# Statistics on ScalarE, a residual added by transfers, an earlier chain of token sums and a split last block

## The chip, the cores and the metric

The kernel runs on one core of a Trainium2 chip. The metric is the device time of one execution in microseconds (us), here the median of several executions. Engines are named as in the profile: PE multiplies matrices (PEld is its weight load), DVE is VectorE, ACT is ScalarE, POOL is GpSimd, SP is SyncE, which here only issues DMA transfers.

## The reference

Two batches of 1024 tokens, D = 1024 columns, all in fp32:

```
xn  = layernorm(x)                               # per token over D
s   = xn @ (weight with 32x32 blocks masked).T + bias
c_b = softmax(Wq @ mean_tokens(xn_b) . keys)     # 8 mixing weights per batch
y   = xn @ (W_org + sum_e c_b[e] * down_e up_e).T
out = x + s * silu(y)
```

## The kernel before, in words

**Precision.** Every fp32 operand is kept as a rounded part and a remainder ("hi" and "lo", made by an ACT cast and a DVE subtraction), and each product is three matmuls: L425, L426, L427 for the batch-0 products, L389, L390, L391 for the mixing of the weights, L1147 for batch 1.

**Order of work.** The order on PE, DVE, ACT and POOL is that of the source, written by hand. Each of these engines runs its instructions in that order. Only SP's queue, from which nearly all loads go out, is ordered by a scheduler. So an instruction that waits holds all that is behind it on its engine.

**Stages.** Batch 0 is worked through in eight tiles of 128 tokens and two halves of 512 output columns:

- a start that loads, normalises and transposes batch 0 and computes the products with half 0 of the masked matrix (`s0`);
- the loop over k that mixes half 0 of the batch-0 matrix `y00`. For each of eight row tiles: `y_prep` splits a tile of the down matrices (`dhi` L380 on ACT, `dlo` L381 on DVE), `y_mul` is 12 matmuls into a `psw` bank (L389 to L391; there are two banks), `y_sum` adds W_org on DVE (L396), `y_hi` (L399, ACT) and `y_lo` (L407, DVE) split the sum. The `cut` tiles (L367 ACT, L368 DVE) are the up matrices times the mixing weights;
- `phase("y", 0, 0, ...)`, eight tiles of 24 matmuls (`gemm`) each followed by a `y_mul` for `y01`; `jobs_b` lists the side work per tile: stores, `mask_part` (block mask sums), `nat_stats` (mean and variance of a batch-1 token tile with two `bn_stats` L144 and an aggregate on DVE), `spread_stats` (spreads them into rows), and the first steps of the wide chain;
- `phase("y", 0, 1, ...)`, eight tiles of 24 matmuls; `jobs_c` makes the rows of `s1`, the other half of the masked matrix (load `ws`, L274 DVE, L277 ACT, L282 DVE), goes on with the wide chain, and computes the mixing weights of batch 1 (`coeffs(1)`);
- `s_tile(0..7)`, eight tiles with `s1`, with the 16 mixing steps of batch 1 (`fold`) between the first five;
- batch 1 by a scheme of seven products per 2x2 block (`quad` over eight units of 84 matmuls, L1147), whose token operands are the sums and differences of token tiles prepared by the wide chain. ACT copies (L1178, L1154 for `s5` and `s2`, L1202) and DVE adds move partial sums between banks. `out_tile` finishes a block (L1124 to L1134).

**The wide chain.** `wide_load(j, half)` loads 512 KB of transposed batch-1 tokens, `wide_a(j)` and `wide_b(j)` normalise the first and the second of a pair, and `wide_b` also forms the sums and stores them to DRAM (`xv`) from POOL's queue. There are four pairs.

**Residuals of batch 0.** For each final tile SP loads the input tile into `res` ahead of the products; after them DVE multiplies by the `stash` (L471) and adds to `res` (L472); `store_late` puts the store on ACT's queue (L480). In batch 1 the same sum is made for most blocks by a transfer of POOL that adds the input to the block in place (L1130), and by a DVE add (L1133) in the last unit.

**The end.** The last unit's three last products go into `pb`, `py` and `pa`, one bank each; each is followed by two 128x512 operations of DVE (L1124, L1133) and a store.

Of the kernel before, what the change touches and what calls it, by code (L numbers as in the profile page):

```python
# [9 lines left out]
F32 = mybir.dt.float32  # L10
# [3 lines left out]
AF = mybir.ActivationFunctionType  # L14
ALU = mybir.AluOpType
# [17 lines left out]
def kernel(  # L33
# [130 lines left out]
    def nat_stats(b, i):  # L164
        t = b * TPB + i
        xn = nat_tile()
        nc.sync.dma_start(xn, x[t * P : (t + 1) * P, :])
        bn(t, xn, 0)
        bn(t, xn, 1)
        rstd_of(t)  # L170

    def group(b, g):
        if (b, g) not in xg:
# [287 lines left out]
            y_evac(mine, ps, b, i)  # L461
        stash[(b, h, i)] = mine

    def final_evac(kind, b, h, i, ps, res):
        t = b * TPB + i
        mine = stage_l.tile([P, NH], F32, name="mine", tag="g", bufs=2)
        if kind == "s":
            s_evac(mine, ps, b, i, h * NH, NH)
        else:
            y_evac(mine, ps, b, i)  # L470
        nc.vector.tensor_tensor(mine, mine, stash[(b, h, i)], ALU.mult)  # L471
        nc.vector.tensor_tensor(res, res, mine, ALU.add)  # L472
        late_stores.append((out[t * P : (t + 1) * P, h * NH : (h + 1) * NH], res))

    late_stores = []

    def store_late():

        while late_stores:
            nc.scalar.dma_start(*late_stores.pop(0))  # L480

    sum_stores = []

# [12 lines left out]
    def phase(kind, b, h, w, final, jobs):  # L496

        for i in range(TPB):
            t = b * TPB + i
            if final:  # L500
                res = stage_l.tile([P, NH], F32, name="res", tag="res", bufs=3)
                nc.sync.dma_start(res, x[t * P : (t + 1) * P, h * NH : (h + 1) * NH])
            flush()
            if (b, h, i) in split_at:
                ps, part = open_gemm(b, i, w)
                part(0, 4)
                split_at[(b, h, i)]()
                part(4, NKT)
            else:
                ps = gemm(b, i, w)  # L510
            if final:
                pending.append(J(final_evac, kind, b, h, i, ps, res))
            else:
                pending.append(J(tile_evac, kind, b, h, i, ps))
            for job in jobs(i):
                job()
# [100 lines left out]
    with tc.manual_schedule(engines={mybir.EngineType.PE, mybir.EngineType.DVE, mybir.EngineType.Activation, mybir.EngineType.Pool}):  # L617
# [208 lines left out]
        for k in range(NKT):  # L826
            y_mul(0, 0, k)
            if k == 0:
                tile_evac("s", 0, 0, 7, q7)
            y_sum(0, 0, k)  # L830
            if k + 2 < NKT:
                y_prep(0, 0, k + 2)
            y_hi(y00, 0, 0, k)
            y_lo(y00, 0, 0, k)

        def mix_jobs(dst, b, h, i):
            if i == 0:
# [13 lines left out]
        def jobs_b(i):  # L851
            if i == 0:
                yield J(scale_up, 0, 1)
            yield J(mix_jobs, y01, 0, 1, i)
            yield J(store_late)
            if i < 4:
                yield J(mask_part, 2 + i // 2, i % 2)
            for t in ((0,), (1, 2), (3, 4), (5,), (6, 7), (), (), ())[i]:
                yield J(nat_stats, 1, t)
            if i == 4:  # L860
                yield J(wide_load, 0, 0)
                yield J(wide_load, 0, 1)
            if i == 5:
                yield J(spread_stats)
                yield J(wide_a, 0)
            if i == 6:
                yield J(wide_b, 0)
            if i == 7:
                yield J(wide_load, 1, 0)
                yield J(wide_load, 1, 1)  # L870


# [20 lines left out]
        def wide_load(j, half):  # L893
            if half == 0:
                pair = lambda n: cupool.tile([P, 2, NH], F32, name=n, tag="cu")
                if j == 0:
                    tt = [stash_p.tile([P, NH], F32, name="tt", tag="stash") for _ in range(2)]
                    wide[0] = pair("ac"), tt, nat_tile().rearrange("p (g n) -> p g n", g=2)
                elif j == 1:
                    ac, bd, tt = pair("ac"), pair("bd"), pair("tt")  # L900
                    wide[1] = ac, [tt[:, 0], tt[:, 1]], bd
                elif j == 2:
                    tt = pair("tt")
                    wide[2] = wide[0][0], [tt[:, 0], tt[:, 1]], wide[0][2]
                else:
                    wide[3] = wide[1]
            kt = j + 4 * half
            t = wide[j][2 * half]
            nc.sync.dma_start(t.rearrange("p g n -> p (g n)"), xT[kt * P : (kt + 1) * P, S : 2 * S])
# [36 lines left out]
        steps = coeffs(1)  # L946

        def jobs_c(i):
            if i == 6:
                yield steps[0]  # L950
                yield steps[1]
            if i == 7:
                yield steps[3]
                yield J(scale_up, 1, 0)
            yield J(s_mul, s1, 1, i)
            yield J(s_lo, s1, 1, i)
            if i in (1, 3):
                yield J(wide_load, (i + 3) // 2, 0)
                yield J(wide_load, (i + 3) // 2, 1)
            if i < 6:  # L960
                yield J((wide_a, wide_b)[i % 2], 1 + i // 2)

        split_at[(0, 1, 7)] = steps[2]
        phase("y", 0, 1, y01, False, jobs_c)


# [38 lines left out]
        ORDER_X = (0, 3, 4, 1, 5, 2, 6)  # L1005

        def s_tile(i):
            res = stage_l.tile([P, NH], F32, name="res", tag="res", bufs=3)
            nc.sync.dma_start(res, x[i * P : (i + 1) * P, NH:])
            store_late()  # L1010
            flush()
            ps = gemm(0, i, s1)
            pending.append(J(final_evac, "s", 0, 1, i, ps, res))

        units = [("s", 0), ("y", 0), ("y", 1), ("s", 1), ("y", 2), ("s", 2), ("y", 3), ("s", 3)]
        opools = [None, None]
# [88 lines left out]
        held = {}  # L1105
        pools_b1 = {}

        def out_tile(u, i, t, ps):

            kind, p = units[u]  # L1110
            n = p + 4 * i
# [1 line left out]
            if u % 2 == 0:  # L1113
# [3 lines left out]
                else:  # L1117
                    nc.scalar.activation(g, ps, AF.Silu)
                gates[(p, i, t)] = g
                return  # L1120
            g = gates.pop((p, i, t))
            res = held.pop((i, t), None)
# [17 lines left out]
                nc.sync.dma_start(res, xT[n * P : (n + 1) * P, S + t * NH : S + (t + 1) * NH])  # L1140
                held[(i, t)] = res

        def product(u, a, m, ps, start, js=range(4)):
            o = ow[u]
            for j in js:
                for k, (wl, xl) in enumerate(((0, 0), (0, 1), (1, 0))):
                    nc.tensor.matmul(  # L1147
                        ps, lhsT=o[:, a, wl, j, :], rhs=xw[j][:, m, xl, :],
                        start=start and j == 0 and k == 0, stop=j == 3 and k == 2, skip_group_check=True,
                    )  # L1150

# [5 lines left out]
        def quad(u, ahead, behind=()):  # L1157
# [41 lines left out]
            slot(3)  # L1199
            product(u, 2, 5, pb, False)  # L1200
            after(4)
            nc.scalar.copy(pa, pb)  # L1202
            nc.vector.tensor_tensor(pb, pb, s5, ALU.add)
            slot(4)
            product(u, 6, 2, py, False)
            out_tile(u, 0, 1, py)
            out_tile(u, 1, 1, pb)
            res_load(u, 1, 0)
            slot(5)
            product(u, 3, 6, pa, False)  # L1210
            out_tile(u, 1, 0, pa)
# [9 lines left out]
        cm_t2, pools_b1["tmp2"] = open_pool("tmp2", 1)  # L1221
        ahead = unit_jobs(1)
        behind = [[J(fill, j, m, xs_pool) for j in (2, 3)] for m in ORDER_X[2:]]
        behind[1].insert(0, store_late)
        quad(0, ahead, behind)
        close(cm_xs)
        cm_t, pools_b1["tmp"] = open_pool("tmp", 1, side="right")
# [59 lines left out]
```

## Time and profile before

| what | value |
|---|---|
| median of 3 executions | 461.38 us (459.7 to 463.19) |
| the profiled execution | 462.08 us |
| its span, first to last instruction | 460.1 us |
| mean granted clock of PE | 0.986 |
| PE, DVE, ACT, POOL busy | 97%, 66%, 37%, 13% |
| instructions | 5752 |
| moved by DMA | 89.52 MB, 195 GB/s on average |
| accumulating transfers of batch 1 | 12 of 256 KB, 6.1 us from issue to landing |
| stores of batch 0 | 16 of 256 KB, 2.7 us |
| loads of `ws` | 8 of 256 KB, 5.5 us |

The span is counted from the first to the last instruction; the execution's time contains it and 1.98 us around it. The busy time of an engine says how much it had to do, not what set the end; that is read from waits, from the chain of work that ended last, and from the granted clock in stretches of the span. A row of a timeline gives start, length, engine, line, operation, output and inputs, and in brackets the engine's idle time just before with what ended it. A matmul of 128x512 shows a length of 0.39 us in a row, but matmuls overlap: the next one starts 0.227 us later.

### The profile page before, as it was taken

How to read it: one execution, taken by the hardware profiler on the slowest of the kernel's cores; microseconds unless marked ns; L12 is line 12 of the kernel's file. 1: busy time of each engine (PE TensorE's matmuls, PEld its weight loads, DVE VectorE, ACT ScalarE, POOL GpSimd, SP SyncE). 2: the span in 40 equal slices, each digit the busy share in tenths (PEclk: the TensorE clock that was granted, in tenths of full speed). 3: DMA queues.
4: the chain of work that ended last, by engine and by line, in shares of the span. 5: the costliest groups of instructions: out<-in, count | busy, mean ns of one | idle time of the engine just before them, and what ended most of it. 6: DMA issues, size and time to landing. Idle time of an engine off the chain costs nothing.

```text
span 460.1 us, 5752 instructions
## 1 busy us (share of the span) xinstructions
PE 444.7 (97%) x2047; PEld 365.4 (79%) x2047; DVE 305.1 (66%) x492; ACT 169.3 (37%) x277; POOL 59.5 (13%) x72
## 2 busy tenths in 40 slices
PE   7799999999999999997999999999999999999995
PEld 5689888888887888885888788877888888888884
DVE  5889778666775788866546776669466294465624
ACT  3576624363323132213324233158243422441510
POOL 3764210000010202230000000000020020002000
PEclk9899999999999999997999999999999999999999
DMA  8995406687862586799778985664274246218003
GB/s 267 390 350 196 146 24 205 183 281 255 287 230 93 186 317 227 277 309 303 243 249 276 297 274 152 207 219 137 79 147 134 85 98 177 91 24 220 31 1 114
DMA packets 47404, 89.52 MB, mean 195 GB/s; under 512 B 4752, under 2 KB 14992, under 8 KB 47376
## 3 DMA queue, kind: packets, MB, share of 16 engines
q1 hardware_dynamic: 32784, 70.28, 46.1%
q0 software_dynamic: 3840, 10.49, 8.9%
q10 hardware_dynamic: 10752, 8.39, 5.7%
q8 instruction: 16, 0.26, 0.2%
q14 instruction: 12, 0.10, 0.1%
HBM read 69.21 MB, written 19.92 MB: 194 GB/s over the span
## 4 chain that ended last, share of the span: by engine, by line
PE 85%; DVE 8%; DMA 4%; issue 1%; ACT 1%; SPq 0%; ACTq 0%; DVEq 0%
PE acc_ps L1147 23%; PE acc_ps L425 11%; PE acc_ps L426 11%; PE acc_ps L427 11%; PE py L1147 9%; PE psw L391 6%; PE psw L389 6%; PE psw L390 6%; DMA ws<-in_wT_dram 2%; DMA raw<-in_x_dram 1%; DVE slot L558 1%; DVE ramp L549 1%; DMA misc<-in_up_dram 1%; DVE st L144 1%; DVE xw L1002 1%
## 5 line engine op out<-in xcount | busy, mean ns | idle before, releaser
L1147 PE MATMUL acc_ps<-xw,ow 128*128 128x512 f32 x480 | 113.6, 393 | 0.4 <-ACT acc_ps L1178 0.4
L425 PE MATMUL acc_ps<-slot,xgrp 128*128 128x512 f32 (+1 forms) x288 | 107.4, 373 | 2.8 <-ACT slot L277 2.7
L426 PE MATMUL acc_ps<-slot,xgrp 128*128 128x512 f32 (+1 forms) x288 | 106.8, 371 | 2.7 <-DVE slot L558 2.7
L427 PE MATMUL acc_ps<-slot,xgrp 128*128 128x512 f32 (+1 forms) x288 | 106.4, 369 | 0.7 <-DVE xgrp L570 0.7
L1147 PEld LDWEIGHTS acc_ps<-xw,ow 128*128 128x128 f32 x480 | 90.0, 188 | 21.3 <-ACT acc_ps L1178 0.8
L426 PEld LDWEIGHTS acc_ps<-slot,xgrp 128*128 128x128 f32 x288 | 54.9, 191 | 12.6 <-DVE slot L558 3.6
L425 PEld LDWEIGHTS acc_ps<-slot,xgrp 128*128 128x128 f32 x288 | 54.8, 190 | 12.3 <-ACT slot L277 3.1
L427 PEld LDWEIGHTS acc_ps<-slot,xgrp 128*128 128x128 f32 x288 | 55.0, 191 | 10.2 <-DVE xgrp L570 1.1
L391 PE MATMUL psw<-cut,dlo 128*128 128x512 f32 x128 | 50.9, 397 | 0.8 <-DVE dlo L381 0.8
L389 PE MATMUL psw<-cut,dhi 128*128 128x512 f32 x128 | 51.0, 399 | 0.0
L390 PE MATMUL psw<-cut,dhi 128*128 128x512 f32 x128 | 50.6, 395 | 0.0
L1147 PE MATMUL py<-xw,ow 128*128 128x512 f32 x192 | 46.9, 392 | 0.0
L1147 PEld LDWEIGHTS py<-xw,ow 128*128 128x128 f32 x192 | 36.1, 188 | 8.1
L1047 DVE TENSOR_TENSOR ow<-raw,ow 128x1024 fp32r<-128x1024 f32 (+1 forms) x32 | 34.5, 1087 | 10.4 <-ACT ow L1046 10.4
L1130 POOL DMA_DIRECT2D gate<-in_xT_dram x12 | 10.5, 906 | 203.0 <-DVE gate L1128 133.9
L380 ACT CAST dhi<-ds 128x512 fp32r<-128x512 f32 x32 | 19.8, 617 | 40.0 <-PE psw L390 23.8
L396 DVE TENSOR_TENSOR wo<-wo,psw 128x512 f32<-128x512 f32 x32 | 22.0, 686 | 18.6 <-PE psw L391 18.5
L1046 ACT CAST ow<-raw 128x1024 fp32r<-128x1024 f32 (+1 forms) x32 | 29.4, 940 | 1.6 <-DVE wo L396 1.6
L391 PEld LDWEIGHTS psw<-cut,dlo 128*128 128x128 f32 x128 | 24.5, 192 | 6.7 <-DVE dlo L381 1.2
L390 PEld LDWEIGHTS psw<-cut,dhi 128*128 128x128 f32 x128 | 24.6, 192 | 5.4
L389 PEld LDWEIGHTS psw<-cut,dhi 128*128 128x128 f32 x128 | 24.6, 192 | 5.2
L1192 DVE TENSOR_TENSOR py<-py,s 128x512 f32<-128x512 f32 x8 | 5.6, 698 | 30.7 <-ACT s L1154 30.7
(160 smaller groups left out, 477.6 us busy)
## 6 DMA issues: line engine op xcount, KB each, us to landing
ds<-in_down_dram SPq DMA_DIRECT2D x32, 256.0 KB, 3.7
wo<-in_worgT_dram SPq DMA_DIRECT2D x32, 256.0 KB, 3.8
raw<-in_x_dram SPq DMA_DIRECT2D x11, 512.0 KB, 6.5
res<-in_x_dram SPq DMA_DIRECT2D x16, 256.0 KB, 3.8
out_dram<-res ACTq DMA_DIRECT2D x16, 256.0 KB, 2.7
raw<-in_wu_dram SPq DMA_DIRECT2D x8, 512.0 KB, 5.1
yu<-wo ACTq DMA_DIRECT2D x16, 256.0 KB, 4.1
xs<-xv SPq DMA_DIRECT2D x16, 256.0 KB, 4.0
```

The source lines that it names most:

```text
L380: nc.scalar.copy(dhi, ds)
L389: nc.tensor.matmul(ps, lhsT=dhi[:, c, :], rhs=u[c][:, 0, :], start=c == 0, stop=False)
L390: nc.tensor.matmul(ps, lhsT=dhi[:, c, :], rhs=u[c][:, 1, :], start=False, stop=False)
L391: nc.tensor.matmul(ps, lhsT=dlo[:, c, :], rhs=u[c][:, 0, :], start=False, stop=c == 3)
L396: nc.vector.tensor_tensor(ws, ws, ps, ALU.add)
L425: nc.tensor.matmul(ps, lhsT=xs[:, kt, 0, cols], rhs=w[:, kt, 0, wc], start=kt == 0, stop=False)
L426: nc.tensor.matmul(ps, lhsT=xs[:, kt, 0, cols], rhs=w[:, kt, 1, wc], start=False, stop=False)
L427: nc.tensor.matmul(ps, lhsT=xs[:, kt, 1, cols], rhs=w[:, kt, 0, wc], start=False, stop=kt == NKT - 1)
L1046: nc.scalar.copy(o[:, a:b, 0], raw[:, a:b])
L1047: nc.vector.tensor_tensor(o[:, a:b, 1], raw[:, a:b], o[:, a:b, 0].bitcast(F32), ALU.subtract)
L1130: nc.gpsimd.dma_start(g, xT[n * P : (n + 1) * P, S + t * NH : S + (t + 1) * NH], accum_op=ALU.add)
L1147: nc.tensor.matmul(ps, lhsT=o[:, a, wl, j, :], rhs=xw[j][:, m, xl, :], start=start and j == 0 and k == 0, stop=j == 3 and k == 2, skip_gro ...
```

## The change

1. `act_stats` computes a batch-1 tile's mean and variance with ACT: a copy that also sums, two small DVE operations for the mean and its negative, a square with the negative mean as bias that also sums, a small DVE operation and POOL's power. Three tiles are done in the y00 loop after k = 2, 4 and 6, two more in tiles 0 and 1 of phase y(0,0); the other three stay with `nat_stats`.
2. `final_evac` multiplies into the stash tile, adds the input by an accumulating DMA from POOL's queue, and `store_out` stores the tile from ACT's queue later. The `res` tiles of batch 0 and their loads are gone.
3. The steps of the wide chain move one tile to the front; its second pair gets other buffers; `coeffs(1)` and `scale_up(1, 0)` move from tiles 6 and 7 to 5 and 6 and `s_mul`/`s_lo` of rows 5 to 7 are all put into tile 5's jobs.
4. In the last unit, the order of the finished blocks is changed and the last product is done in two halves of 256 columns in two banks, each half with its own two DVE operations and store.

```
+    def act_stats(i):
+        t = TPB + i
+        xn = nat_tile()
+        nc.sync.dma_start(xn, x[t * P : (t + 1) * P, :])
+        sm = small.tile([P, 2], F32, name="sm2")
+        nc.scalar.activation(xn, xn, AF.Copy, accum_out=sm[:, 0:1])
+        m = small.tile([P, 2], F32, name="mean1", bufs=5)
+        nc.vector.tensor_scalar(m[:, 0:1], sm[:, 0:1], 1.0 / D, None, ALU.mult)
+        nc.vector.tensor_scalar(m[:, 1:2], sm[:, 0:1], -1.0 / D, None, ALU.mult)
+        nc.scalar.activation(xn, xn, AF.Square, bias=m[:, 1:2], accum_out=sm[:, 1:2])
+        ve = small.tile([P, 1], F32, name="ve", bufs=3)
+        nc.vector.tensor_scalar(ve, sm[:, 1:2], 1.0 / D, EPS, ALU.mult, ALU.add)
+        nc.gpsimd.tensor_tensor(rstd[:, t : t + 1], ve, mhalf, ALU.pow)
+        means[t] = m[:, 0:1]
...
-        nc.vector.tensor_tensor(mine, mine, stash[(b, h, i)], ALU.mult)
-        nc.vector.tensor_tensor(res, res, mine, ALU.add)
-        late_stores.append((out[t * P : (t + 1) * P, h * NH : (h + 1) * NH], res))
+        res = stash[(b, h, i)]
+        nc.vector.tensor_tensor(res, res, mine, ALU.mult)
+        t = b * TPB + i
+        at = slice(t * P, (t + 1) * P), slice(h * NH, (h + 1) * NH)
+        nc.gpsimd.dma_start(res, x[at], accum_op=ALU.add)
+        out_stores.append((out[at], res))
...
             y_hi(y00, 0, 0, k)
             y_lo(y00, 0, 0, k)
+            if k in (2, 4, 6):
+                act_stats(k // 2 - 1)
... jobs_b
-            yield J(store_late)
+            yield J(store_out, 1)
             if i < 4:
                 yield J(mask_part, 2 + i // 2, i % 2)
-            for t in ((0,), (1, 2), (3, 4), (5,), (6, 7), (), (), ())[i]:
+            if i < 2:
+                yield J(act_stats, 3 + i)
+            for t in ((), (5,), (6,), (7,), (), (), (), ())[i]:
                 yield J(nat_stats, 1, t)
+            if i == 3:
+                yield J(wide_load, 0, 0)
             if i == 4:
-                yield J(wide_load, 0, 0)
                 yield J(wide_load, 0, 1)
-            if i == 5:
                 yield J(spread_stats)
                 yield J(wide_a, 0)
+            if i == 5:
+                yield J(wide_b, 0)
+                yield J(wide_load, 1, 0)
             if i == 6:
-                yield J(wide_b, 0)
+                yield J(wide_a, 1)
             if i == 7:
-                yield J(wide_load, 1, 0)
                 yield J(wide_load, 1, 1)
... jobs_c
-            if i == 6:
+            if i < 2:
+                yield J(store_out, 1 - i)
+            if i == 5:
                 yield steps[0]
                 yield steps[1]
-            if i == 7:
+            if i == 6:
                 yield steps[3]
-                yield J(scale_up, 1, 0)
-            yield J(s_mul, s1, 1, i)
-            yield J(s_lo, s1, 1, i)
-            if i in (1, 3):
-                yield J(wide_load, (i + 3) // 2, 0)
-                yield J(wide_load, (i + 3) // 2, 1)
+                yield J(scale_up, 1, 0, up_homes)
             if i < 6:
-                yield J((wide_a, wide_b)[i % 2], 1 + i // 2)
-        split_at[(0, 1, 7)] = steps[2]
+                yield J(s_mul, s1, 1, i)
+                yield J(s_lo, s1, 1, i)
+            if i == 5:
+                for kt in (6, 7):
+                    yield J(s_mul, s1, 1, kt)
+                    yield J(s_lo, s1, 1, kt)
+            if i in (0, 2):
+                yield J(wide_load, 2 + i // 2, 0)
+                yield J(wide_load, 2 + i // 2, 1)
+            if i < 5:
+                yield J((wide_b, wide_a)[i % 2], 1 + (i + 1) // 2)
+        split_at[(0, 1, 6)] = steps[2]
... quad, last unit
+                out_tile(u, 1, 1, pb)
+                res_load(u, 1, 0)
+                product(u, 6, 2, py, False)
+                out_tile(u, 0, 1, py)
+                for c, pc in halves:
+                    product(u, 3, 6, pc, False, cols=c)
+                    out_tile(u, 1, 0, pc, c)
+                return
... quad(0)
-        behind[1].insert(0, store_late)
+        behind[2].insert(0, store_out)
```

## The prediction

> **What bounds the kernel now.** I read the page's first section, then the windows of each stage, the chain that ended last, and last the timelines of the engines at the edited places.
>
> ```profile
> PE 444.7 (97%) x2047; PEld 365.4 (79%) x2047; DVE 305.1 (66%) x492; ACT 169.3 (37%) x277; POOL 59.5 (13%) x72
> ...
> L425 PE MATMUL acc_ps<-slot,xgrp 128*128 128x512 f32 (+1 forms) x288 | 107.4, 373 | 2.8 <-ACT slot L277 2.7
> ```
>
> The matmul engine is busy in all but 15 us. The change removes no product, so it can win only what the matmul engine waits or runs slowly, some of the 15 us and the tail, and it can lose wherever it makes that engine wait. The second line already names the largest single wait, 2.7 us behind L277, a row of the matrix s1. The windows show it with what it drags behind it (columns: stretch, its length, busy time and count of PE, PEld, DVE, ACT, POOL, then granted clock, DMA share, GB/s):
>
> ```profile
> 205.00:210.00 5.00, 5.00 (x23) 3.85 (x21) 3.61 (x8) 2.68 (x4) 0.08 (x1) 1.00 1.02 393
> 210.00:215.00 5.00, 2.27 (x6) 1.50 (x6) 2.61 (x5) 2.23 (x4) 0.00 (x0) 0.71 0.89 268
> 215.00:220.00 5.00, 5.00 (x15) 3.95 (x14) 2.52 (x5) 0.62 (x1) 0.00 (x0) 0.60 0.65 211
> ```
>
> The granted clock falls to a half after the wait. A 128x512 matmul follows the one before it after 0.23 us at full clock and 0.43 at half, as the chain that ended last shows (start, us, what):
>
> ```profile
> 200.81 0.61 DVE ws L274
> ...
> 202.82 8.54 DMA ws<-in_wT_dram
> 211.38 0.70 DVE ws L274
> 212.11 0.63 ACT slot L277
> 212.74 0.04 issue
> 212.78 0.80 PE acc_ps L425
> ...
> 218.57 0.43 PE psw L389
> ...
> 219.26 0.23 PE psw L391
> ```
>
> The last ws tile was issued at 202.82, took 8.54 us beside 393 GB/s of other loads, and after two casts s_tile(0) could go on. The matmul before it started at 209.66, so its slot ended at 209.89: 2.89 us idle. From 212.4 to 219.0 the engine issued 15 matmuls in 6.56 us, where full clock takes 15 x 0.227 = 3.40: 3.16 lost. Together 6.05 us.
>
> **Part 1: token pairs one tile sooner.** Now jobs_c runs the chain wide_a, wide_b, each over one 512 KB load, to tile 5 of phase y(0,1); it ends at 198.8, 38.3 us after that phase began at 160.5, and ws, coeffs(1) and its wu loads crowd behind it. In the built order one pair more is done in phase y(0,0), the chain has five steps left, and bd(1), issued behind the last y_mul of y(0,0), lands about 5.2 us into the phase. From there five steps and the s_mul and s_lo between them are 27.7 us of DVE work by their rows: end at +32.9, 5.4 sooner. The ws loads of rows 5 to 7 are then issued at +29.5 to +30.3 and land, at 5.5 to 8.54 us each, at +35 to +39. Rows 5 to 7, soft and the cuts follow in DVE's order; the first dlo of y(1,0) comes out at +49.0 to +50.5 and is wanted at +50.15. So 0 to 2 us of wait remain, I take 0.3, and with a wait that short the clock loss goes too: -5.7 (-4 to -6.05).
>
> **Part 2: residual by accumulating transfers.** Sixteen res loads leave SP and sixteen adds of 0.69 us leave DVE (11.1 us); sixteen accumulating DMAs come onto POOL, and each store on ACT now waits for one. The nearest row is batch 1's accumulates (line, engine op, count, KB each, median us to landing):
>
> ```profile
> gate<-in_xT_dram POOLq DMA_DIRECT2D x12, 256.0 KB, 6.1
> ```
>
> Each also holds POOL about 0.91 us to issue (L1130). In y(0,0) a tile is 8.16 us, and ACT and POOL are mostly idle: nothing lost, since a store is issued one tile late. In the folds one matmul wait can be read, 0.78 us at 255.4 to 256.2, where dlo (L381) came late on DVE right behind the res add of 252.51. One add less in that chain shrinks it by 0.69: -0.7 (0 to -0.8).
>
> The price lies in quad(0). There the store of tile 7 stands in ACT's order ahead of two fills and of the copy s2, and product(2,5), which writes the bank that s2 reads, waits for s2.
>
> ```profile
> 299.55 1.56 PE L1147 MATMUL acc_ps<-xw,ow 128*128 128x512 f32 x6
> ...
> 305.72 7.61 PE L1147 MATMUL acc_ps<-xw,ow 128*128 128x512 f32 x31 [0.41 <-ACT acc_ps L1178]
> ```
>
> ```profile
> 307.60 0.58 ACT L1154 COPY s<-py 128x512 f32<-128x512 f32 x1
> 309.64 1.25 ACT L1001 CAST xw<-xs 128x512 fp32r<-128x512 f32 x2 [1.46 <-DMA xs<-xv]
> 310.80 0.58 ACT L1154 COPY s<-acc_ps 128x512 f32<-128x512 f32 x1
> ```
>
> Tile 7's last matmul starts at 299.32; its product with the stash is done near 304.3, and at 6.1 us the accumulate lands at 310.4 (4.6 to 8.6 us seen, less part of the issue: 309.3 to 313). Then two fills of 0.62 each and the copy of 0.58: s2 at 312.3 to 312.9 in the middle case, where product(2,5) wants it at 311.16, 24 matmuls after 305.72. +1.75 (0.3 to 4). What is late next is DVE's py add behind s2; units after it don't feel it, as they refill in 19 us.
>
> **Part 3: five statistics on ScalarE.** DVE loses ten bn_stats of 0.68 and five aggregates of 0.21, 7.85 us, none of it where PE waits today, so no gain. ACT gains per tile a Copy with sum over 128x1024, 1.05 + 0.18 (row L579), and a Square with sum that no row shows at that size: between 1.05 (that row) and 2 x 0.51 + 0.19 = 1.21 (L596, 128x256, scaled at most to 4 x 0.51 = 2.04). I take 1.05 + 0.19, the nearest width. DVE gains three small operations of about 0.16 each, in its order between one y_lo and the next y_sum, and they wait for ACT. Queued behind them are y_sum (frees psw), y_prep's dlo, and y_lo. So a loop pass with act_stats holds DVE: 0.68 until y_sum is read, 0.52 y_hi, 1.05 + 0.18 Copy, 0.16 mean, 1.05 + 0.19 Square, 0.15 ve: about 4.0 us instead of the 2.0 (y_sum, dlo, y_lo) of a plain pass, while PE needs 2.72 per pass. Two passes: 6.0 against 5.44. The lateness of y_sum(3), (5), (7) is then 1.3, 1.9, 2.4. What before left as slack is read here:
>
> ```profile
> 86.52 0.69 DVE L396 TENSOR_TENSOR wo<-wo,psw 128x512 f32<-128x512 f32 x1 [0.65 <-PE psw L391]
> 87.12 0.69 DVE L381 TENSOR_TENSOR dlo<-ds,dhi 128x512 fp32r<-128x512 f32 x1
> ...
> 91.96 0.69 DVE L396 TENSOR_TENSOR wo<-wo,psw 128x512 f32<-128x512 f32 x1 [0.65 <-PE psw L391]
> 93.33 0.69 DVE L407 TENSOR_TENSOR slot<-wo,slot 128x512 fp32r<-128x512 f32 x1 [0.69 <-ACT slot L399]
> 93.96 2.74 DVE L368 SCALAR_TENSOR_TENSOR cut<-us,c,cut 128x512 fp32r<-128x512 f32 x4
> 96.62 0.68 DVE L381 TENSOR_TENSOR dlo<-ds,dhi 128x512 fp32r<-128x512 f32 x1
> ```
>
> dlo(7) ended at 87.8 and was wanted at 89.65: the first 1.9 are covered. But everything behind y_sum(7) moves by 2.4: the four cuts to 96.4-99.0 and the first dlo of y01 to 99.7, while its matmul comes at 97.9: 1.84 us idle. From there the second dlo, the fourth act_stats, y_sum, the 1.28 us table load and the mask sums run in one ACT order; gemm(2) of y(0,0) starts near 111.3 instead of 108.5. From tile 2 on DVE has room. Cost +2.7 (1.3 to 4; nothing if the Copy and Square overlap better than their order says).
>
> Whether 1.84 us idle halves the clock too: windows of 3.4 us with PE busy 1.05 (209.0 to 212.4) and 1.24 us (14.4 to 17.8) were followed by half clock, the 0.78 us wait was not. 1.84 in such a window leaves 1.57 busy, near the first if it falls into one, well away if it straddles two; I take no halving, and 3.2 (the same loss as at 212) for the far end.
>
> [...]
>
> **Part 4: last block in two banks.** Now the end is, after the last product:
>
> ```profile
> 455.26 0.76 DVE gate L1124
> 456.01 0.02 issue
> 456.04 0.69 DVE rest L1133
> ```
>
> then a 256 KB store, to 460.1. Two halves are 24 x 0.12 = 2.88 us of matmuls instead of 2.72, and after the second half the two operations are 128x256: 0.42 (row L439) and about 0.45 against 1.45, and half the bytes stored. -0.5 (0 to -0.8).
>
> **The sum.** -5.7 - 0.7 + 1.75 + 2.7 - 0.5 = -2.45. The profiled execution took 462.08 (span 460.1 and 1.98 around it): 459.6. The median of the runs is 0.70 lower, so 458.9 as a median. The measurement tells about 1% (4.6 us) from no change.
>
> **Rivals.** A, the handshakes are hidden: the Copy ends sooner, the accumulate lands at the short end. For it: ACT is 37% busy. Against: strict order on DVE in the loop. 461.38 - 5.7 - 0.7 + 0.3 + 0.3 - 0.5 = 455.1. B, the other side: DVE, held behind ACT in the y00 loop, starves y01's first y_mul by more than about 2 us in one window, and half clock follows. It decides from about 2.2 us of wait in one window (1.2 busy, as at 14.4), which a Square of 1.2 instead of 1.05 us, three times over, brings about. For it: the two windows above and L596 scaled; against: a wait that straddles two windows. 458.9 + 0.4 + 3.2 = 462.5; with the far end of part 3, 463.4. C, the change doesn't do what it says: ws rows 5 to 7 stand behind two wu loads as the last one does now, s_tile(0) or its dlo waits as long as before: 461.38 - 0.7 + 1.75 + 2.7 - 0.5 = 464.6; beyond that, over 466 with halving at both places.
>
> **How the numbers follow.** Forecast 0.40, A 0.23, B 0.23, C 0.14. Predicted 458.9. The range 455 to 465 reaches to A's and C's values. Faster by over 1% (under 456.8): A, and the forecast's low end, 0.27. Slower (over 466.0): B and C with both ends against them, 0.15. Within: 0.58.
>
> **What would show it.** Right: no wait behind L277's successor near 210 and clock 1.0 there; a DVE wait for ACT in the y00 loop and about 1.8 us PE idle near 98; an ACT store in quad(0) waiting for POOL's transfer, and PE waiting at product(2,5); the last DVE pair at 0.4 each. Wrong: no PE wait near 98 (part 3 overpriced), half clock near 100 (B), or a wait of over 2 us before the first fold (C).

## The result, and the profile after

| | before | changed |
|---|---|---|
| median, first series | 461.79 us (20 executions) | 460.27 us (20 executions) |
| ratio, first series | | 0.9968 (95%: 0.9945 to 0.9991) |
| median, second series | 462.01 us (29) | 460.21 us (12) |
| ratio, second series | | 0.9954 (95%: 0.9927 to 0.9982) |
| profiled execution, span | 462.08 us, 460.1 us | 457.88 us, 456.2 us |

The change brings 0.3 to 0.5%: 1.5 to 1.8 us, where 2.45 were forecast. Executions of one kernel lie up to 6 us apart within a series. The mean granted clock accounts for about half of that (squared correlation of time and granted clock 0.50 over the 32 executions of the changed kernel); at one and the same clock, 0.996, fourteen of them took 458.1 to 461.9. The profiled execution of the changed kernel had no half clock (1.000) and is one of its fastest, so its span flatters it by about 1.35 us against that of before, which has a half-clock stretch near its start.

First section of the page of the changed kernel, with the row of batch 1's matmuls from the fifth:

```profile
PE 441.5 (97%) x2059; PEld 362.5 (79%) x2059; DVE 288.1 (63%) x473; ACT 180.1 (39%) x298; POOL 73.7 (16%) x88
...
L1190 PE MATMUL acc_ps<-xw,ow 128*128 128x512 f32 (+1 forms) x492 | 114.2, 388 | 2.0 <-ACT s L1197 1.6
```

DVE lost 17 us of work, ACT gained 11 and POOL 14. None of that is time. The largest wait of before, 2.7 us behind L277, has no row any more; 1.6 us behind a copy to `s` (L1197, the `s2` of quad(0)) is new. The windows that held the wait and the half clock, of the changed kernel:

```profile
205.00:210.00 5.00, 5.00 (x24) 4.14 (x23) 3.54 (x9) 3.70 (x7) 0.36 (x1) 1.00 0.71 247
210.00:215.00 5.00, 5.00 (x24) 4.09 (x23) 2.86 (x5) 1.38 (x3) 0.98 (x1) 1.00 0.82 275
215.00:220.00 5.00, 5.00 (x24) 4.14 (x23) 3.07 (x5) 2.15 (x4) 0.00 (x0) 1.00 0.89 192
```

PE is busy throughout, at clock 1.00. The timeline of DVE in the y00 loop (start, us, engine, line, operation, and the idle time before with its releaser) shows the handshake:

```profile
77.01 0.69 DVE L412 TENSOR_TENSOR wo<-wo,psw 128x512 f32<-128x512 f32 x1 [0.65 <-PE psw L407]
...
79.44 0.15 DVE L180 TENSOR_SCALAR mean<-sm 128x1 f32<-128x1 f32 x1 [0.36 <-ACT raw L178]
79.51 0.14 DVE L181 TENSOR_SCALAR mean<-sm 128x1 f32<-128x1 f32 x1
81.02 0.15 DVE L184 TENSOR_SCALAR ve<-sm 128x1 f32<-128x1 f32 x1 [1.37 <-ACT raw L182]
81.10 0.69 DVE L412 TENSOR_TENSOR wo<-wo,psw 128x512 f32<-128x512 f32 x1
...
93.25 0.69 DVE L412 TENSOR_TENSOR wo<-wo,psw 128x512 f32<-128x512 f32 x1
94.62 0.69 DVE L423 TENSOR_TENSOR slot<-wo,slot 128x512 fp32r<-128x512 f32 x1 [0.69 <-ACT slot L415]
95.25 2.74 DVE L384 SCALAR_TENSOR_TENSOR cut<-us,c,cut 128x512 fp32r<-128x512 f32 x4
97.90 0.69 DVE L397 TENSOR_TENSOR dlo<-ds,dhi 128x512 fp32r<-128x512 f32 x1
```

From one y_sum (77.01) to the next (81.10) a pass with `act_stats` takes 4.09 us. DVE stands still for 0.36 and 1.37 us of it behind ScalarE. y_sum(7) comes at 93.25 where a step of 2.72 from 77.01 gives 90.61: 2.64 late. The matmul engine then, at the joint to y01:

```profile
96.19 0.39 PE L443 MATMUL acc_ps<-slot,xgrp 128*128 128x512 f32 x1
97.61 0.50 PE L405 MATMUL psw<-cut,dhi 128*128 128x512 f32 x1 [1.03 <-ACT dhi L396]
97.95 0.40 PE L406 MATMUL psw<-cut,dhi 128*128 128x512 f32 x1
98.64 0.50 PE L407 MATMUL psw<-cut,dlo 128*128 128x512 f32 x1 [0.30 <-DVE dlo L397]
```

A smaller loss stands before it, in the last pass of the loop, where y_mul(7) waits for the bank that the late y_sum(5) frees:

```profile
88.01 0.47 PE L405 MATMUL psw<-cut,dhi 128*128 128x512 f32 x1 [0.16 <-DVE wo L412]
```

Quad(0) of the changed kernel, first on PE, then on ACT:

```profile
300.41 5.87 PE L1190 MATMUL acc_ps<-xw,ow 128*128 128x512 f32 x24 [0.37 <-ACT acc_ps L1221]
307.88 1.43 PE L1190 MATMUL acc_ps<-xw,ow 128*128 128x512 f32 x5 [1.59 <-ACT s L1197]
```

```profile
305.82 0.34 ACTq L506 DMA_DIRECT2D out_dram<-stash  x1
306.20 1.14 ACT L1039 CAST xw<-xs 128x512 fp32r<-128x512 f32 x2 [3.40 <-DMA xs<-xv]
307.25 0.58 ACT L1197 COPY s<-acc_ps 128x512 f32<-128x512 f32 x1
```

Store, two fills, s2, in the order foretold. That the store alone is the cause is what the picture suggests; experiment 5 shows that it is not. The end, from the chain that ended last:

```profile
449.16 2.88 PE acc_ps L1190 x24
...
452.07 0.49 DVE gate L1159
452.57 0.02 issue
452.59 0.42 DVE rest L1160
```

**Where the difference lies.** Laying the starts of the same instructions of both profiles side by side (y_sum, the copies `s5` and `s2`) gives the gain or loss of each stage. The sum is the 3.9 us between the spans. Of the first row, 1.27 us arise between the two matmuls that start at 18.11 and 26.47 before, a stretch that holds the half clock of before (17.57 to 20.98).

| stage | start of the changed kernel against before, at its two ends | difference | forecast |
|---|---|---|---|
| start, nearly all clock | 0 to -1.35 | -1.35 | none |
| y00 loop and phase y(0,0) | -1.35 to +1.34 | +2.69 | +2.7 |
| phase y(0,1), wait near 210 | +1.34 to -4.64 | -5.98 | -5.7 |
| folds | -4.60 to -5.38 | -0.78 | -0.7 |
| first half of quad(0) | -5.38 to -3.55 | +1.83 | +1.75 |
| other units | -3.54 to -3.28 | +0.26 | none |
| end | -3.28 to -3.9 | -0.6 | -0.5 |

Without the first row it is -2.6 against the -2.45 of the sum.

### The profile page after: what moved, and what is told of

It is laid out like the page before. It is cut to its first block, busy times and chain, and to the rows that moved or that the text cites. A ratio compares the mean times of both kernels' runs of the same rounds, so it can differ in the third digit from the quotient of the medians.

```text
span 456.2 us, 5789 instructions
## 1 busy us (share of the span) xinstructions
PE 441.5 (97%) x2059; PEld 362.5 (79%) x2059; DVE 288.1 (63%) x473; ACT 180.1 (39%) x298; POOL 73.7 (16%) x88
## 4 chain that ended last, share of the span: by engine, by line
PE 50%; issue 31%; DVE 7%; POOL 5%; DMA 3%; ACT 3%; SPq 0%; ACTq 0%; POOLq 0%; DVEq 0%
PE acc_ps L1190 23%; PE py L1190 9%; PE acc_ps L443 4%; PE acc_ps L441 4%; PE acc_ps L442 4%; POOL xv L513 2%; POOL stash L491 2%; PE psw L407 2%; PE psw L406 2%; PE psw L405 2%; DMA stash<-in_x_dram 1%; DMA raw<-in_x_dram 1%; DVE slot L580 1%; DVE wo L412 1%; DVE ramp L571 1%
## 5 line engine op out<-in xcount | busy, mean ns | idle before, releaser
L1190 PE MATMUL acc_ps<-xw,ow 128*128 128x512 f32 (+1 forms) x492 | 114.2, 388 | 2.0 <-ACT s L1197 1.6
L442 PEld LDWEIGHTS acc_ps<-slot,xgrp 128*128 128x128 f32 x288 | 54.3, 188 | 12.5 <-DVE slot L580 3.6
L443 PEld LDWEIGHTS acc_ps<-slot,xgrp 128*128 128x128 f32 x288 | 54.2, 188 | 10.2 <-DVE xgrp L592 1.1
L441 PEld LDWEIGHTS acc_ps<-slot,xgrp 128*128 128x128 f32 x288 | 54.3, 188 | 9.2 <-DVE stash L455 0.3
L405 PE MATMUL psw<-cut,dhi 128*128 128x512 f32 x128 | 50.1, 391 | 1.2 <-ACT dhi L396 1.0
L407 PE MATMUL psw<-cut,dlo 128*128 128x512 f32 x128 | 50.5, 394 | 0.3 <-DVE dlo L397 0.3
L406 PE MATMUL psw<-cut,dhi 128*128 128x512 f32 x128 | 50.1, 391 | 0.0
L491 POOL DMA_DIRECT2D stash<-in_x_dram x16 | 14.4, 897 | 120.9 <-DVE stash L488 120.9
L405 PEld LDWEIGHTS psw<-cut,dhi 128*128 128x128 f32 x128 | 24.0, 188 | 7.0 <-ACT dhi L396 2.0
L406 PEld LDWEIGHTS psw<-cut,dhi 128*128 128x128 f32 x128 | 24.0, 188 | 5.3
```

The costliest lines, as they stand in the source:

```text
L405: nc.tensor.matmul(ps, lhsT=dhi[:, c, :], rhs=u[c][:, 0, :], start=c == 0, stop=False)
L406: nc.tensor.matmul(ps, lhsT=dhi[:, c, :], rhs=u[c][:, 1, :], start=False, stop=False)
L407: nc.tensor.matmul(ps, lhsT=dlo[:, c, :], rhs=u[c][:, 0, :], start=False, stop=c == 3)
L441: nc.tensor.matmul(ps, lhsT=xs[:, kt, 0, cols], rhs=w[:, kt, 0, wc], start=kt == 0, stop=False)
L442: nc.tensor.matmul(ps, lhsT=xs[:, kt, 0, cols], rhs=w[:, kt, 1, wc], start=False, stop=False)
L443: nc.tensor.matmul(ps, lhsT=xs[:, kt, 1, cols], rhs=w[:, kt, 0, wc], start=False, stop=kt == NKT - 1)
```

## The experiments

A gain below is read from such offsets where it can be, since the medians carry a spread of some 1 us. The page of each kernel has its own line numbers.

**1. The changed kernel again.**

> The changed kernel once more, unchanged, for a second execution's profile. Theory (the clock gate makes the spread between runs): where the mean granted clock is below 1.0 the half clock stands either in the first 25 us or in the 3.4 us after the wait near 97, each costing 1.2 to 1.7 us; the waits themselves (1.0 and 0.3 near 97, 1.6 near 307) are the same within 0.1. Rival (the spread comes from the transfers): the waits differ by over 0.5 us and the clock explains less than half of the difference.

Span 455.5, clock 1.000; 460.21 us median. The waits came out as 1.05 and 0.30 near 97 and 1.38 in quad(0), and a wait of 0.55 stood in the folds, where the first profile had none. So the waits at 97 are fixed and the others vary by 0.2 to 0.55. The largest difference between the two profiles lies at the start: the first has a wait of 0.93 us near 11.6 that the second lacks, and y_sum(0) comes 1.09 sooner in the second, both at full clock. This profile had no half-clock stretch, so it does not show what one costs. Over both series, six of the 32 executions had clock 1.000, and they took 456.9 to 457.9; the other 26 took 457.9 to 462.9. With half of the variance left over, the theory that the clock alone makes the spread is not shown.

**2. Statistics back on DVE** (part 3 undone).

```
-            if k in (2, 4, 6):
-                act_stats(k // 2 - 1)
...
-            if i < 2:
-                yield J(act_stats, 3 + i)
-            for t in ((), (5,), (6,), (7,), (), (), (), ())[i]:
+            for t in ((0, 1), (2, 3), (4, 5), (6, 7), (), (), (), ())[i]:
```

> Part 3 alone undone: the batch-1 statistics are all on DVE again, two tiles in each of the first four tiles of phase y(0,0), the rest as changed. Theory (DVE held behind ScalarE in the y00 loop, 2.5 us): y_sum is on time in the loop, the wait near 97 is gone, phase y(0,1) starts 2.3 to 2.5 us sooner against the start of the loop, and the time falls by about 2.3. Rival (DVE's own load): the two statistics of 1.64 us per tile hold DVE in phase y(0,0) instead, waits of over 1 us appear between 100 and 135, and the time falls by less than 1 us.

456.71 us median, ratio to before 0.9906 (0.9873 to 0.9940): 3.5 us under the changed kernel's median of the same series. Its profile began with more half clock than the second profile of the changed kernel; against that one it stands at +3.71 in the y00 loop and at +1.13 at the start of phase y(0,1): 2.58 us gained, and no wait over 0.33 in between. (The medians' 3.5 is more than that; with six executions the spread covers the difference.) DVE at the joint:

```profile
93.23 0.69 DVE L412 TENSOR_TENSOR wo<-wo,psw 128x512 f32<-128x512 f32 x1 [0.65 <-PE psw L407]
...
97.89 0.69 DVE L397 TENSOR_TENSOR dlo<-ds,dhi 128x512 fp32r<-128x512 f32 x1
100.42 0.69 DVE L397 TENSOR_TENSOR dlo<-ds,dhi 128x512 fp32r<-128x512 f32 x1 [1.85 <-ACT dhi L396]
101.03 1.28 DVE L144 BATCH_NORM_STATS2 st<-raw 128x6 f32<-128x512 f32 x2
```

y_sum waits for PE again, not the other way round, and the statistics go where DVE would stand idle. The theory holds; the rival doesn't.

**3. ScalarE's statistics drawn apart.**

```
             y_hi(y00, 0, 0, k)
+            if k in (1, 3, 5):
+                early = act_steps(k // 2)
+                early[0]()              # copy with sum, on ScalarE
+            if k in (2, 4, 6):
+                early[1]()              # the two means, on DVE
+                early[2]()              # square with sum, on ScalarE
             y_lo(y00, 0, 0, k)
+            if k in (3, 5, 7):
+                last[3]()               # variance on DVE, power on POOL
+            if k in (2, 4, 6):
+                last = early
-            if k in (2, 4, 6):
-                act_stats(k // 2 - 1)
```

> The three ScalarE statistics of the y00 loop stay on ScalarE, but their copy, means, square and last step are put one loop pass apart each (copy after y_hi of k = 1, 3, 5; means and square in the next pass; the last small step in the pass after), so that DVE finds ScalarE's result there already. Theory (it is the handshake, not ScalarE's work): lateness of y_sum(3), (5), (7) falls from 1.3, 2.0, 2.6 to under 0.3, the wait near 97 is gone, -2.2 us. Rival (ScalarE's 2.4 us per tile hold dhi and y_hi themselves): y_sum stays over 1 us late by k = 7 and the wait near 97 stays over 0.8 us; under -1.

459.16 us median. In the loop the theory holds: against the second profile of the changed kernel y_sum(7) came 2.62 sooner (+2.66 to +0.04), and the wait near 97 is gone, though ScalarE does all its work. But only 1.24 us are left at the start of phase y(0,1): a new wait of 1.02 us near 109, behind `r`, an operation of DVE in the mask sums, which comes after the fourth tile's statistics. That one is still in one piece:

```profile
102.58 0.15 DVE L190 TENSOR_SCALAR mean<-sm 128x1 f32<-128x1 f32 x1 [1.40 <-ACT raw L185]
...
104.23 0.15 DVE L200 TENSOR_SCALAR ve<-sm 128x1 f32<-128x1 f32 x1 [1.44 <-ACT raw L195]
104.37 0.69 DVE L428 TENSOR_TENSOR wo<-wo,psw 128x512 f32<-128x512 f32 x1
```

The expected 2.2 overlooked this second handshake. That it makes the wait at `r` is read from these rows; no run draws it apart alone.

**4. Four tiles in the loop instead of three.**

```
-            if k in (2, 4, 6):
-                act_stats(k // 2 - 1)
+            if k in (2, 3, 4, 6):
+                act_stats((2, 3, 4, 6).index(k))
```

(and only the fifth in phase y(0,0), at tile 1)

> A dose: four ScalarE statistics in the y00 loop (after k = 2, 3, 4, 6) instead of three, the fourth taken from tile 0 of phase y(0,0). Theory (each pass with act_stats holds DVE 4.1 us against 2.72): y_sum(7) is 1.35 us later again, the wait near 97 grows from 1.35 to about 2.7 in sum, and the clock is halved for 3.4 us after it: +1.4 +1.5 there, less what tile 0 gains. Rival (the wait doesn't follow the number of passes, as the slack of the loop takes it up): it grows by less than 0.5.

463.18 us median, ratio to before 1.0046 (1.0016 to 1.0075) where the changed kernel, in another series, had 0.9954: some 4 us slower by the ratios. By offsets against the second profile of the changed kernel it is +2.20 at y_sum(7) and +2.15 at the start of phase y(0,1). The cost follows the number of passes, but not where expected: with the slack used up, y_mul itself waits for a free psw bank, 0.89 and 1.00 us near 87 and 91, and the wait near 97 stays at 1.13 and 0.30. This profile shows no half clock there. What makes the rest of the 4 us was not looked for.

**5. The last stores put behind s2.**

```
-        behind[2].insert(0, store_out)
+        behind[3].insert(0, store_out)
```

> The last two stores of batch 0 are put on ScalarE's queue one product later in quad(0), behind the copy s2. Theory (the store's wait for the accumulating transfer holds s2): the store waits no longer, s2 starts about 1.7 us sooner, and the 1.6 us wait of the matmul engine at the fifth product of quad(0) is gone; -1.6 us, and nothing new. Rival (the two fills ahead of s2 wait for their own xs loads anyway): s2 moves by less than 0.5 us and at least 1 us of the wait stays.

460.75 us median, and the theory that the store is what holds s2 falls. No store stood ahead of s2, and the wait was 1.76 us; that is what the rival foretold. ACT in quad(0) of this kernel:

```profile
306.20 0.58 ACT L1197 COPY s<-py 128x512 f32<-128x512 f32 x1
309.99 1.21 ACT L1039 CAST xw<-xs 128x512 fp32r<-128x512 f32 x2 [3.21 <-DMA xs<-xv]
310.60 0.82 ACTq L506 DMA_DIRECT2D out_dram<-stash  x2
311.11 0.58 ACT L1197 COPY s<-acc_ps 128x512 f32<-128x512 f32 x1
```

ACT waited 3.21 us for the loads of the two fills. (The two stores stand behind s2 in the program. Their rows begin while the casts still run, and s2 follows the casts with no idle time.) The DMA issues of the stretch in which they were issued (303.0 to 304.8; queue, count, KB, us to landing), and then the same pair of loads before, with two plain stores beside it (304 to 307):

```profile
xs<-xv SPq DMA_DIRECT2D x2, 256.0 KB, 6.3
stash<-in_x_dram POOLq DMA_DIRECT2D x1, 256.0 KB, 6.8
```

```profile
out_dram<-res ACTq DMA_DIRECT2D x2, 256.0 KB, 4.0
xs<-xv SPq DMA_DIRECT2D x2, 256.0 KB, 4.0
```

The two loads are 2.3 us slower, and an accumulating transfer runs beside them, that of tile 7. A new theory follows: it shares the DMA engines with them.

This does not clear the store of the changed kernel, though. There the store's issue ends at 306.16 (305.82 and 0.34), the first cast starts at 306.20, and s2 at 307.25. The two loads landed at 305.98 and 306.50, and s2 starts 0.54 us after the second landing in this experiment (310.57, 311.11), which would have been 307.04. So store and loads hold s2 to within 0.2 us of each other, and by these rows either alone would leave nearly the whole wait.

**6. Tile 7 the old way, the other fifteen by transfer.**

```
+            src = None
+            if i == 7:
+                src = misc[:, 0, :]
+                nc.sync.dma_start(src, x[i * P : (i + 1) * P, NH:])
...
+        if src is None:
             nc.gpsimd.dma_start(res, x[at], accum_op=ALU.add)
+        else:
+            nc.vector.tensor_tensor(src, src, res, ALU.add)
+            res = src
```

> Of the changed kernel, only the last tile of batch 0 takes the old way (its input loaded ahead, here into a part of misc, and added on DVE); the other fifteen keep the accumulating transfer. After the last experiment the first theory of the wait in quad(0) (the store on ScalarE's queue) has fallen. Theory now (the accumulating transfer of tile 7 shares the DMA engines with the fills' loads and makes two of them 2 us longer): without it the loads of the fourth pair land in about 4.0 us instead of 5.3 to 6.3, s2 starts 1.6 us sooner, and the 1.4 to 1.8 us wait is gone; -1.6 us, more where the wait had halved the clock. Rival (the earlier arrival of quad(0), which leaves less time for fills): the loads keep 5 us or more and at least 1 us of the wait stays.

458.60 us median, ratio to before 0.9935 (0.9911 to 0.9959), an interval that overlaps that of the changed kernel; by offsets 1.74 us gained in quad(0) (+3.00 to +1.26 against the second profile of the changed kernel). The fills' loads, in the stretch from 301.5 to 303.5, and s2 on ACT:

```profile
xs<-xv SPq DMA_DIRECT2D x2, 256.0 KB, 2.9
```

```profile
305.73 1.27 ACT L1043 CAST xw<-xs 128x512 fp32r<-128x512 f32 x2 [0.28 <-DMA xs<-xv]
306.91 0.58 ACT L1205 COPY s<-acc_ps 128x512 f32<-128x512 f32 x1
```

The wait at the fifth product is gone. quad(0) follows the folds here as closely as in the changed kernel (16.16 us from the last y_sum to its first matmul in both), so the rival falls. With no store and no accumulating transfer beside them the two loads take 2.9 us, beside two plain stores 4.0 (before), beside one accumulating transfer 6.3 (experiment 5): it is not any transfer of this size that costs so much. That the DMA engines are what they share is still an inference.

**7. The reverse: the kernel before with this one transfer.** Tile 7's residual alone goes by an accumulating transfer, and its store is issued two products later.

> The kernel before with a single accumulating transfer, that of the last tile of batch 0, whose store comes two products later than before, so that no instruction ahead of s2 waits for it. Theory (DMA engines shared with the fills' loads): the loads beside it take 5.3 us or more instead of 4.0, and the matmul engine waits 1.3 to 1.8 us at the fifth product of quad(0), where before it doesn't wait; nothing else moves. Rival (the wait came with the other parts, which bring quad(0) on sooner or move loads): no wait over 0.3 us there.

The two loads beside it took 6.2 us each, the casts ahead of s2 waited 3.03 us for them on ACT, and the matmul engine waited 1.76 at the fifth product:

```profile
311.85 1.24 ACT L1014 CAST xw<-xs 128x512 fp32r<-128x512 f32 x2 [3.03 <-DMA xs<-xv]
```

In this execution, the slowest of its twelve (465.37 us), half clock followed as well:

```profile
311.40:314.80 3.40, 1.64 (x8) 1.00 (x7) 2.30 (x4) 2.94 (x6) 0.00 (x0) 0.97 0.60 198
314.80:318.20 3.40, 3.40 (x10) 2.69 (x9) 3.33 (x7) 2.57 (x4) 0.00 (x0) 0.53 0.40 139
```

so that quad(0) lost 3.4 us in all (offsets +0.30 to +3.72). The medians don't show it: 461.89 us, ratio 1.0005 (0.9978 to 1.0032). The trace decides for the mechanism; what it costs on average is known only to these bounds. They end at +1.5 us, so a wait of 1.76 in every execution would have to be paid back in part elsewhere.

**8. Part 2 alone on the kernel before.**

> The kernel before with part 2 alone: all sixteen residuals of batch 0 by accumulating transfers. Theory (the transfers cost nothing in the phases, but the one of tile 7 stands beside the fills' loads): the wait at the fifth product of quad(0) appears, 1.4 to 1.8 us; the fold's wait near 255 has no fixed size (0 to 1.2 in the runs so far) and is no reliable gain; all in all +1 to +2 against before. Rival (fewer loads on SP and fewer adds on DVE help the stages before): the wait near 210 shrinks by over 1 us and the whole is faster than before.

466.15 us median, ratio 1.0108 (1.0073 to 1.0143), 4.5 us slower; +1 to +2 was expected. Quad(0) has its wait (2.00 us, +2.2 by offsets). The rest is in phase y(0,1), +1.8 by offsets: PE waits 1.03 near 202 and 4.55 near 211, with half clock for 3.4 us behind the longer wait where before has 6.8. What the trace offers as the cause stands on ACT at that phase's first tile:

```profile
161.21 0.69 ACT L448 ACTIVATE mine<-acc_ps,rstd 128x512 f32<-128x512 f32 x1
166.60 0.34 ACTq L490 DMA_DIRECT2D out_dram<-stash  x1
167.03 0.62 ACT L277 CAST slot<-ws 128x512 fp32r<-128x512 f32 x1 [5.13 <-DMA stash<-in_x_dram]
```

The store waits for its accumulating transfer, which takes 9.5 us beside three 512 KB loads (7.6 to 11.1 us each; the same loads took 6.7 to 8.1 before), and holds the cast of `ws` behind it; DVE's wide chain starts its second pair at 168.30 instead of 165.94. This is the wait that was foretold for quad(0), at another place. The slower loads can delay the chain too, and no run separates the two. In the changed kernel, whose wide loads are issued at other times, the store is issued at 162.85 and nothing waits for it.

**9. Half of part 1 undone:** `coeffs(1)`, `scale_up(1, 0)` and rows 5 to 7 back in tiles 5 to 7; the wide chain stays sooner.

> Of part 1, the second half is undone in the changed kernel: coeffs(1), scale_up(1, 0) and rows 5 to 7 of s1 go back to tiles 5, 6 and 7 of phase y(0,1); the wide chain stays one tile sooner. Theory (the chain's end sets when rows 6 and 7 and the mixing weights come): DVE is free of the chain at +33, so rows 6 and 7 come out in time though later, the mixing weights' cuts end about 5 us later, and the first dlo of the folds makes the matmul engine wait about 3 to 5 us near 208 with a half clock after it; slower than the changed kernel by 4 to 7 us. Rival (the earlier chain alone removes the wait): the change is under 1 us.

461.33 us median, ratio to before 1.0004 (0.9974 to 1.0034) where the changed kernel, in another series, had 0.9954: 2.3 us slower by the ratios, +1.5 by offsets:

```profile
214.44 0.50 PE L441 MATMUL acc_ps<-slot,xgrp 128*128 128x512 f32 x1 [0.78 <-ACT slot L293]
215.17 0.50 PE L442 MATMUL acc_ps<-slot,xgrp 128*128 128x512 f32 x1 [0.23 <-DVE slot L298]
```

The wait for the last row of s1 is back, at 1.0 instead of 2.7 us, and with no half clock behind it. So the earlier chain alone takes 4.5 of the 6 us, and the moved rows the other 1.5. The 3 to 5 us that were expected, at the first dlo of the folds, were too many and at another place; the rival's "under 1" was too little.

**10. Both repairs:** statistics on DVE, tile 7 the old way.

> Both repairs: all statistics on DVE in phase y(0,0), and tile 7 the old way. Theory: the two costs are apart in time, so the gains add: 1.6 us under the kernel with the statistics on DVE alone, near 455, no wait of over 0.6 us between 60 and 450 but the fold's near 250, and a clock of 0.995 or more, since no wait after the start is long enough to halve it. Rival (one repair lets another wait grow): over 456.5.

454.61 us median, ratio to before 0.9861 (0.9825 to 0.9898), faster than both kernels. No wait from 60 us on is over 0.54. The clock of its executions was 0.992 to 0.998, where 0.995 or more was expected. Against before it stands at -2.48 in the y00 loop (the start, half clock included), again -2.48 at the start of phase y(0,1), and -8.48 behind the old wait near 210: the whole 6 us and no price.

**11. The same with the old end.**

> The best version so far (statistics on DVE, tile 7 the old way) with part 4 undone: the last block in one bank, as before. Theory (two banks shorten what follows the last matmul by about 0.8 us and lengthen the matmuls by 0.16): from the last matmul's end to the span's end 4.9 us instead of 4.2, +0.6 in the trace; the medians can't tell it. Rival (the end is set by the store's landing alone): under 0.2 in the trace.

From the last matmul's end (its start, and 12 or 24 steps of 0.227 or 0.12) to the span's end: 446.48 + 2.72 to 454.2, 5.0 us, against 443.44 + 2.88 to 450.6, 4.3 us. Part 4 is worth about 0.6 with the longer matmuls. The median was 456.64, ratio to before 0.9900 (0.9866 to 0.9934), against 0.9861 in experiment 10: 1.8 us by the ratios, more than the trace explains, but from six executions each, in different series and with intervals that overlap.

## Why the prediction was right

The medians came out 1.3 to 1.4 us above the 458.9 forecast, in a range (455 to 465) so wide that no change at all would have lain in it too. So the terms are the test, and not all of them held for the reason given.

**Part 1** held: -5.98 against -5.7, and the clock loss went with the wait. Its steps came as well, counted from the start of the phase at 161.78: the chain ended at +33.7 (+32.9 forecast), the last three `ws` loads landed at +35.2 to +38.0 (+35 to +39), and the first dlo was done at +48.9 (+49.0 to +50.5), 1.7 us before its matmul.

**Part 3** held in its total and in DVE's steps, and less well in where PE paid. A pass took 4.09 us (4.0 forecast), y_sum(3), (5), (7) were 1.37, 2.01, 2.64 late (1.3, 1.9, 2.4), and the stage lost 2.69 (2.7). The Square took 1.15 plus the read of its sum, where 1.05 had been taken from the copy's row. At the joint, the wait was put on dlo alone at 1.84 us; measured are 1.03 for dhi and 0.30 for dlo, and the stretch between the two gemms was 1.9 us longer than before. But the forecast put the other 0.9 behind that, before gemm(2), and there nothing was lost. Instead 0.55 was lost ahead of it (the offset of gemm(0)), at y_mul(7)'s bank, where the sum had no wait, and 0.2 later in the phase; that these add up to nearly the same is luck. Experiment 2 undoes the cause and regains 2.58.

**Part 2, quad(0)**: the size was right (+1.75, measured +1.83) and the step was incomplete. It said that tile 7's store, waiting on ACT for its accumulating transfer (6.1 us forecast, 6.39 measured), holds s2. In the changed kernel's rows it does, but experiment 5 removes that order and the wait stays; 7 has the wait with the store out of the way, since the transfer itself lengthens the two fill loads beside it from 4.0 to 6.2 us. The sum had put that at nothing. Both causes end within 0.2 us of each other, so the sum was right with one of them left out. Experiment 6 takes both away and can't tell them apart; that the store alone would hold s2 as long is what the rows say, and no run shows it.

**Part 2, folds**: -0.7 was forecast and -0.78 is in the first profile, yet without the add the wait there was 0.55, 0.38, 1.21, 1.01, 0.99, 1.07, 0.54 and 0.69 in the profiles of experiments 1, 3, 4, 5, 6, 8, 10 and 11 (before: 0.78; with the adds of before but for tile 7's, in experiment 7: 1.09); it was absent in the first profile and in 2 and 9. So the removed add is not what sets it. What does was not tried; the term was luck.

**Part 4** held: -0.6 against -0.5.

**Rivals.** A would have needed the handshakes hidden; experiment 10, which has none, shows about what that is worth, 454.6 against the 455.1 given to A. B's half clock did not follow the wait near 97 in the six profiles that have it. It did follow the 1.8 us wait of quad(0) in two profiles and not in others with waits of 1.3 to 2.0, so in these runs the length of the wait alone did not decide it. The traces show one thing more. In each of them the ends of the half-clock stretches lie whole multiples of 3.413 us apart (before: 17.57, 20.98, 212.12 and 218.95, the last three 1, 57 and 59 multiples behind the first). On that grid, the stretch just before the half clock held 1.65 us of matmuls in experiments 2 and 7. The wait of 1.72 us in experiment 4 left 1.69 in its stretch and the clock stayed full, and the 2.00 us of experiment 8 were split over two stretches with 2.28 and 2.55. The wait near 97, in its two parts, left 1.98 to 2.38. The prediction's windows of 3.4 us are as long as the first half-clock stretch of before (17.57 to 20.98); that the busy time in one decides was its author's estimate. The two with 1.05 and 1.24 busy lie 0.2 to 0.3 us off that grid; on it they hold 1.34 and 1.48. So 1.84 us in one stretch, 1.57 busy, would have been closer to half clock than the forecast took it to be; the wait came out shorter and in two parts instead. This is a reading of the waits of quad(0), not a measured threshold: near the start, with other shapes of matmul, a stretch with 1.62 busy (experiment 5) kept the full clock and one with 1.93 (experiment 9) lost it. C's wait is gone, and experiment 9 shows a quarter of its loss (1.5 of 6 us) when its rows are late.

## What to carry to other kernels

Work moved to an idle engine can still cost the busy one if the two exchange small results inside one step (here passes of 4.09 us where PE needs 2.72, and 2.58 us regained in experiment 2): draw the exchange apart over steps, or leave the work where the engine stands idle anyway. A transfer's price can also be paid by the loads beside it (4.0 to 6.2 us in experiment 7), so look at the time to landing of neighbours, and not only at who waits for the transfer itself. When a sum and a trace agree on the size and the place of a wait, one experiment that takes away the supposed cause alone is still needed: here a second cause stood behind the first, of the same length to within 0.2 us by the rows.

## What the runs showed of the hardware that was not expected

- An accumulating transfer of 256 KB slowed two 256 KB loads beside it from 4.0 to 6.2 us (experiment 7), or to 6.3 (experiment 5) from 2.9 with neither a store nor an accumulating transfer beside them (experiment 6). Beside three 512 KB loads it took 9.5 us itself, and they took 7.6 to 11.1 instead of 6.7 to 8.1 before (experiment 8).
- The clock went to half after waits of 1.76 and 1.77 us in two executions (7 and 2), and stayed full after 2.00 in another (8).
- Executions of the kernel before with 0.984 to 1.000 of the clock took 457.4 to 465.1 us. The clock accounts for about half of that spread (squared correlation 0.49 over 72 executions), which is what a comparison of medians has to see through.
